# Half of an output projection by seven block products for eight, both token halves together

## The chip, the cores and the metric

The kernel runs on one core of one Trainium2 chip. The metric is the device time of one execution in microseconds (us), as the median of several runs. Profiles show one execution; its engines are named PE (TensorE, matrix products), DVE (VectorE), ACT (ScalarE), POOL (GpSimd) and SP (SyncE, which issues nearly all DMAs here).

## The reference

One decoder layer over 8 sequences of 100 tokens with 1024 features, in float32. Three blocks follow one another, each added to its input and normalised: `x = layernorm(x + block(x))`.

- Retention: 8 heads with 128 features for queries and keys and 256 for values and gates. Its end is what the change touches:

```
o = einsum('bhij,bjhd->bihd', scores, v)
o = o * rsqrt(mean(o*o) + EPS) * g_norm_weight
o = o * (g * sigmoid(g))
return o.reshape(B, T, H * DV) @ Wo          # (800 x 2048) @ (2048 x 1024)
```

- Cross attention with 16 query heads and 4 key/value heads over 722 context tokens and the causal 100 own ones.
- A gated feed-forward block with 4096 hidden features.

## The kernel before

All activations lie with features on the 128 partitions and tokens along the free axis. The 800 tokens are two halves of `N` = 400 (four sequences each), which is the width of nearly every matmul. A float32 operand is split into a high and a low part in the format that TensorE takes (`split2`, L66: a copy on ACT, L67, and a subtraction on DVE, L68); a product of two such operands is three matmuls (`mm3`, L85 to L88: high by high, high by low, low by high).

Weights come through `load_w` (L70): a 512 KB load into one of three `wst` buffers and a split into one of four `w` buffers. The four `big` buffers (L163) hold activations of whichever stage runs.

`seven` (L342) multiplies a 2 x 2 block matrix of weights by a 2 x 2 block matrix of activations with seven block products instead of eight (Winograd's form of Strassen's scheme). The activations' blocks are two feature groups by the two token halves; it needs the operands `b11`, `b21`, `b22` and four mixed ones, `t1` to `t4`, ready and split. The mixtures of the weights are made in the kernel on DVE (L375 to L378). With `into` the results are added on DVE straight into given rows (L360, L369). It is a generator that yields between products, and `in_turn` (L408) interleaves neighbouring units. The retention's projections of heads 1 to 7 and the feed-forward run through it already; one unit is 7 products x 4 x 3 = 84 matmuls.

The retention core of head h (`core`, L475) leaves two tiles `oo[half]`, each with the head's two feature blocks. `gated` (L505) scales them by the root and the gate, splits them and writes high and low parts to the DRAM tensor `o1d` (L516, L517).

The output projection (`out_proj`, L216) runs over the two token halves in turn. `load_o1` (L562) reads the eight heads of one half from `o1d` into four `big` tiles. For each of the 8 row blocks `m` of the result, 16 k tiles accumulate in one PSUM bank: two weight loads (`c` 0: heads 0 to 3, `c` 1: heads 4 to 7) and 48 matmuls. In half 0 the first four row blocks go together, `c` 0 before `c` 1, so that the last heads are needed late. The residual row is added by DVE (L239), the sum for the mean is carried along (L254).

The layer norm of half 0 (`norm_root`, L276, then `scaled`, L269) runs while half 1 is multiplied. For half 1 the mean is taken early, from seven of eight row blocks (`norm_early`, L291, its matmul on L294), while the last row block is multiplied, and corrected by `norm_more` and `norm_late`. The results are the split tiles `z1[half]`, from which the next stage projects queries, keys and values: first four query blocks of half 0, then of half 1. All four `w` buffers are taken by these four blocks. `load_context(0)` (L579) fills the four `big` tiles again in the same stretch, through the `wst` buffers.

The order on each engine is not the program's. A planner runs through the kernel with its own model of times and puts instructions down as they become ready, the earlier ones of the program first; buffers are given out in the same pass. Each engine then works its list off in that order, and SP issues its DMAs in that order too.

Of the kernel before, what the change touches and what calls it, by code (L numbers as in the profile page):

```python
# [8 lines left out]
F32 = mybir.dt.float32  # L9
FR = mybir.dt.float32r  # L10
# [6 lines left out]
P = 128  # L17
# [22 lines left out]
def decoder_layer(ctx, tc, xT, cT, w1, wo1, w2, wo2, wc, w3, wd, gw, qw, kw, trig, dec, mask, out):  # L40
    nc = tc.nc

    def sbuf(name, bufs, side=None):
        return tc.tile_pool(name=name, bufs=bufs, side=side, reuse_waits="tile")
# [21 lines left out]
    def split2(hi, lo, src):  # L66
        nc.scalar.copy(hi, src)  # L67
        nc.vector.tensor_tensor(lo, src, f32(hi), ALU.subtract)  # L68

    def load_w(src, w=None, parts=1):  # L70
        st = wp.tile([P, KT * P], F32, tag="wst", name="wst", bufs=3)
        if w is None:
            w = wp.tile([P, 2, KT * P], FR, tag="w", name="w", bufs=4)
        for i in range(parts):
            c = slice(i * KT * P // parts, (i + 1) * KT * P // parts)
            nc.sync.dma_start(out=st[:, c], in_=src[:, c])
            split(w[:, :, c], st[:, c])
        return w
# [17 lines left out]
    def acc_tag():  # L96
        turn[0] += 1
        return "as"[turn[0] % 2]
# [66 lines left out]
    def big(shape):  # L165
        return bp.tile(shape, FR, tag="big", name="big")
# [49 lines left out]
    def out_proj(half, w, load_o, res, yp, ybufs, p, make_z, dst, after=None):  # L216

        og = load_o(half)
        y = yp.tile([P, KT, N], F32, tag="y", name="y", bufs=ybufs)
        s1 = p.tile([P, N], F32, tag="s1", name="s1", bufs=2)  # L220
        first = 4 if half == 0 else 1
        for ms in [range(first)] + [[m] for m in range(first, KT)]:
            if half == 1 and KT - 1 in ms:
                early = norm_early(y, s1, p)
            accs = [bank(("aaasaaaa", "sssaaass")[half][m])[:, :N] for m in ms]
            for c in range(2):
                for m, acc in zip(ms, accs):
# [24 lines left out]
    def add_up(s1, y, m):  # L252
        if m > 0:
            nc.vector.tensor_tensor(s1, y[:, 0] if m == 1 else s1, y[:, m], ALU.add)  # L254
# [36 lines left out]
    def norm_early(y, s1, p, first=KT - 1):  # L291
        n = y.shape[2]
        mean = bank("s")[:, :n]
        nc.tensor.matmul(mean, onem7, s1, start=True, stop=True)  # L294
# [125 lines left out]


    with sbuf("l1", 2) as p:
# [82 lines left out]
        def gated(h, g):  # L505

            ln_exp()
            rs = [inv_root(p, ss[half], eps_o, pin=True) for half in range(2)]
            for half, r in enumerate(rs):
                t = oo[half]  # L510
                nc.vector.tensor_tensor(t, t, r[:, None, :].to_broadcast([P, 2, N]), ALU.mult)
                for blk in range(2):
                    nc.vector.tensor_tensor(t[:, blk], t[:, blk], g[half, blk], ALU.mult)
                of = p.tile([P, 2, N], FR, tag="of", name="of", bufs=1)
                split2(of, t, t)
                nc.sync.dma_start(out=f32(o1d[h, :, half, :, 0]), in_=f32(of))  # L516
                nc.sync.dma_start(out=f32(o1d[h, :, half, :, 1]), in_=t)  # L517

        def silu(acc, t=None):
            t = temp() if t is None else t  # L520
# [41 lines left out]
    def load_o1(half):  # L562
        t = [big([P, 2, 2, 2, N]) for _ in range(4)]
        for h in range(NH1):
            nc.sync.dma_start(out=f32(t[h // 2][:, h % 2]), in_=f32(o1d[h, :, half]))
        return lambda k: (t[k // 4][:, k // 2 % 2, k % 2, 0], t[k // 4][:, k // 2 % 2, k % 2, 1])
# [363 lines left out]
    class rows:  # L930
# [144 lines left out]
```

## Time and profile before

| | |
|---|---|
| median of 3 runs | 2516.33 us (2516.01 to 2520.12) |
| profiled execution | 2517.7 us, span 2515.9 us |
| mean granted TensorE clock | 0.993 |
| instructions | 37158, of which 14036 matmuls |
| busy: TensorE, VectorE, ScalarE, GpSimd | 2465.4, 1992.2, 1343.5, 481.2 us |
| DMA | 433.96 MB, 172 GB/s over the span |
| first and last matmul of the output projection | 436.9 and 585.5 us |

The profile lists instructions by line and by the program's tile names, without buffer numbers: `a<-big,w` is a matmul into a PSUM bank with the tag `a` that reads a `big` and a `w` tile. Matmuls overlap, so their durations (0.34 us) are longer than the step from one to the next. A name in angle brackets behind an instruction says what ended the engine's idle time before it.

### The profile page before, as it was taken

Reading aid. Unit: us, or ns where it says so; the run is one execution under the profiler, and the core shown is the slowest. Engines: PE = TensorE matmul, PEld = TensorE weight load, DVE = VectorE, ACT = ScalarE, POOL = GpSimd, SP = SyncE. Lnnn points to the kernel's source line nnn. Section 1 sums busy time; section 2 is a strip of 40 time slices with the busy share of each in tenths; the row PEclk is TensorE's granted clock in tenths of the full one; section 3 lists DMA queues with packets and bytes.
Section 4 is the critical chain, followed back from the end, with each engine's and each line's share of the span. In section 5 each row is a group of like instructions: output and inputs, shape, how many; then the busy total and the mean of one; then the engine's idle time right before and its main releaser. Section 6 shows DMA issues by size and latency. Waiting matters only on the chain.

```text
span 2515.9 us, 37158 instructions
## 1 busy us (share of the span) xinstructions
PE 2465.4 (98%) x14036; PEld 2442.0 (97%) x14036; DVE 1992.2 (79%) x3110; ACT 1343.5 (53%) x2264; POOL 481.2 (19%) x234
## 2 busy tenths in 40 slices
PE   8999999999899999999999999999999999999997
PEld 8999999999899999999999999999999999998997
DVE  7678876568989798899999999866987777666656
ACT  6667676335767565556566566533544544432221
POOL 0111111002645334433433433100000000000000
PEclk9999999999999999999999999999999999999999
DMA  7334445774444654554554554574455445388731
GB/s 240 110 110 127 136 144 187 239 266 148 144 152 133 207 175 142 178 166 151 169 176 144 166 192 135 189 273 152 145 181 192 159 160 167 127 302 311 250 102 53
DMA packets 224450, 433.96 MB, mean 172 GB/s; under 512 B 47338, under 2 KB 168042, under 8 KB 211854
## 3 DMA queue, kind: packets, MB, share of 16 engines
q1 hardware_dynamic: 223118, 427.39, 50.7%
q0 software_dynamic: 1152, 4.19, 1.1%
q8 instruction: 110, 1.80, 0.3%
q14 instruction: 70, 0.57, 0.1%
HBM read 322.18 MB, written 109.35 MB: 172 GB/s over the span
## 4 chain that ended last, share of the span: by engine, by line
PE 89%; DVE 6%; ACT 1%; DMA 1%; issue 1%; SPq 0%; DVEq 0%; ACTq 0%
PE a L88 18%; PE a L86 18%; PE a L87 18%; PE s L88 9%; PE s L87 9%; PE s L86 9%; PE v L88 2%; PE v L86 2%; PE v L87 2%; PE s L491 1%; PE s L688 1%; DVE r L120 1%; DVE r L119 1%; PE s L148 1%; DMA tp<-in_xT 1%
## 5 line engine op out<-in xcount | busy, mean ns | idle before, releaser
L86 PE MATMUL a<-big,w 128*128 128x400 f32 (+2 forms) x1808 | 611.4, 339 | 11.7 <-ACT big L67 7.4
L87 PE MATMUL a<-big,w 128*128 128x400 f32 (+2 forms) x1808 | 611.1, 338 | 0.0
L88 PE MATMUL a<-big,w 128*128 128x400 f32 (+2 forms) x1808 | 609.7, 338 | 0.0
L67 ACT CAST w<-wst 128x1024 fp32r<-128x1024 f32 (+1 forms) x231 | 239.2, 1038 | 389.4 <-PE s L88 130.7
L68 DVE TENSOR_TENSOR w<-wst,w 128x1024 fp32r<-128x1024 f32 (+1 forms) x231 | 281.0, 1218 | 117.0 <-ACT w L67 115.1
L86 PEld LDWEIGHTS a<-big,w 128*128 128x128 f32 x1808 | 341.3, 189 | 13.3 <-ACT big L67 7.7
L87 PEld LDWEIGHTS a<-big,w 128*128 128x128 f32 x1808 | 342.0, 189 | 1.3 <-DVE big L68 0.3
L88 PEld LDWEIGHTS a<-big,w 128*128 128x128 f32 x1808 | 342.0, 189 | 0.9 <-DVE w L68 0.2
L86 PE MATMUL s<-big,w 128*128 128x400 f32 x664 | 230.6, 347 | 0.1
L87 PE MATMUL s<-big,w 128*128 128x400 f32 x664 | 229.2, 345 | 0.0
L88 PE MATMUL s<-big,w 128*128 128x400 f32 x664 | 229.1, 346 | 0.0
L125 POOL PARTITION_ALL_REDUCE ss<-sq x56 | 161.1, 2881 | 336.3 <-DMA zd<-y 167.0
L605 POOL PARTITION_ALL_REDUCE kss<-ksq x64 | 173.2, 2706 | 116.4 <-ACT ksq L604 115.7
L86 PE MATMUL a<-z,w 128*128 128x400 f32 x488 | 168.6, 346 | 8.0 <-ACT r L118 4.3
L88 PE MATMUL a<-z,w 128*128 128x400 f32 x488 | 169.4, 348 | 0.7 <-DVE w L68 0.7
L87 PE MATMUL a<-z,w 128*128 128x400 f32 x488 | 169.4, 347 | 0.0
L87 PE MATMUL s<-z,w 128*128 128x400 f32 x400 | 139.1, 348 | 2.4 <-DVE z L68 2.4
L86 PE MATMUL s<-z,w 128*128 128x400 f32 x400 | 139.9, 350 | 0.0
L88 PE MATMUL s<-z,w 128*128 128x400 f32 x400 | 139.4, 348 | 0.0
L722 ACT ACTIVATE s<-s,rk 128x400 f32<-128x400 f32 x160 | 87.7, 591 | 91.9 <-DVE sm L742 65.5
L86 PEld LDWEIGHTS s<-big,w 128*128 128x128 f32 x664 | 124.6, 188 | 1.4 <-ACT w L67 0.4
L87 PEld LDWEIGHTS s<-big,w 128*128 128x128 f32 x664 | 124.6, 188 | 1.1
(330 smaller groups left out, 5650.9 us busy)
## 6 DMA issues: line engine op xcount, KB each, us to landing
wst<-in_w SPq DMA_DIRECT2D x135, 512.0 KB
w<-wcd SPq DMA_DIRECT2D x64, 1024.0 KB
wst<-in_wo SPq DMA_DIRECT2D x64, 512.0 KB
hd<-h SPq DMA_DIRECT2D x12, 1400.0 KB
wst<-in_wd SPq DMA_DIRECT2D x64, 256.0 KB
big<-o1d SPq DMA_DIRECT2D x16, 800.0 KB
qd<-d SPq DMA_DIRECT2D x32, 400.0 KB
q<-qd SPq DMA_DIRECT2D x32, 400.0 KB
```

The costliest lines, as they stand in the source:

```text
L67: nc.scalar.copy(hi, src)
L68: nc.vector.tensor_tensor(lo, src, f32(hi), ALU.subtract)
L86: nc.tensor.matmul(acc, lh, rh, start=start, stop=False, skip_group_check=chain)
L87: nc.tensor.matmul(acc, lh, rl, start=False, stop=False, skip_group_check=chain)
L88: nc.tensor.matmul(acc, ll, rh, start=False, stop=stop, skip_group_check=chain)
L119: nc.vector.scalar_tensor_tensor(q, ss, eps, q, ALU.add, ALU.mult)
L120: nc.vector.scalar_tensor_tensor(q, q, 3.0, r, ALU.subtract, ALU.mult)
L125: nc.gpsimd.partition_all_reduce(y, x, P, op)
L148: nc.tensor.transpose(tr[0:T, b * P:(b + 1) * P], vt[:, b * T:(b + 1) * T], ident)
L491: nc.tensor.matmul(bt(o)[:, b], vv[:, b * P:(b + 1) * P], pf[:, b], start=True, stop=True)
L605: nc.gpsimd.partition_all_reduce(ss[:, at], sq[:, at], P, RED.add)
L722: nc.scalar.activation(sc, sp, AF.Copy, scale=rk[:, c:c + 1])
```

## The change

The k range of the output projection is cut in two.

Heads 0 to 3 keep eight block products: `by_eight` multiplies one token half by their weights, 24 matmuls for each row block, and adds each result to a row that was loaded beforehand with the residual. For half 0 it runs in front, for half 1 at the end. Their weights are loaded once for each half.

Heads 4 to 7 go through `seven`, both token halves together, in four `rows_unit`s of two row blocks each, between the two. The feature blocks of the 2 x 2 scheme are the two 128-feature blocks of a head, and the four heads are the four k tiles of each block product. For these heads `gated` no longer splits. It makes the mixed operands `t1` to `t4` with four subtractions and writes the seven unsplit operands, head by head, to the new DRAM tensor `o1m`. The seven operand tiles are read back during the front half, one after each row block, and split in place. Four of them use the buffers that later hold `z1`, two are `big` tiles, one is a tile of its own.

All rows of the result, of both halves, now lie in four tiles `yt` that are filled with the residual first and added to in three steps. The sums for the mean of half 0 are made after the units. The last row block of half 1, behind which the early mean is taken, has 24 matmuls instead of 48.

```diff
-    o1d = dr.tile([NH1, P, 2, 2, 2, N], FR, name="o1d")
+    o1d = dr.tile([QT, P, 2, 2, 2, N], FR, name="o1d")
+    o1m = dr.tile([7, P, QT, N], F32, name="o1m")
...
                 for blk in range(2):
                     nc.vector.tensor_tensor(t[:, blk], t[:, blk], g[half, blk], ALU.mult)
+                if h >= QT:
+                    continue
                 of = p.tile([P, 2, N], FR, tag="of", name="of", bufs=1)
                 split2(of, t, t)
                 nc.sync.dma_start(out=f32(o1d[h, :, half, :, 0]), in_=f32(of))
                 nc.sync.dma_start(out=f32(o1d[h, :, half, :, 1]), in_=t)
+            if h < QT:
+                return
+
+            b1, b2 = oo[0], oo[1]
+            t1, t2, t4, t3 = g[0, 0], g[1, 1], g[0, 1], b2[:, 0]
+            nc.vector.tensor_tensor(t1, b2[:, 0], b1[:, 0], ALU.subtract)
+            nc.vector.tensor_tensor(t3, b2[:, 1], b2[:, 0], ALU.subtract)
+            nc.vector.tensor_tensor(t2, b2[:, 1], t1, ALU.subtract)
+            nc.vector.tensor_tensor(t4, b1[:, 1], t2, ALU.subtract)
+            to = lambda a, n: o1m[a:a + n, :, h - QT].rearrange("c p n -> p c n")
+            nc.sync.dma_start(out=to(0, 2), in_=b1)
+            nc.sync.dma_start(out=to(2, 2), in_=b2)
+            for i, t in enumerate((t1, t2, t4)):
+                nc.sync.dma_start(out=o1m[4 + i, :, h - QT], in_=t)
...
-        z1 = [out_proj(half, wo1, load_o1, xT, p, 2, p, lambda _: [z1p.tile([P, 2, QT, N], FR, tag="z", name="z")
-                                                                 for _ in range(2)], zd) for half in range(2)]
...
+    def by_eight(y, w, og, half, s1, p, load=None):
+
+        early = None
+        for m in range(KT):
+            if half == 1 and m == KT - 1:
+                early = norm_early(y, s1, p)
+            wt = load_w(w(m))
+            if load is not None:
+                load(m)
+            acc = bank(acc_tag())[:, :N]
+            for k in range(KT):
+                rh, rl = og(k)
+                a = acc if len(rh.shape) == 2 else bt(acc)
+                mmw(a, wt, k, rh, rl, k == 0, k == KT - 1)
+            if early:
+                nc.vector.scalar_tensor_tensor(y[:, m], early[0], -early[2], y[:, m], ALU.mult, ALU.add)
+            nc.vector.tensor_tensor(y[:, m], y[:, m], acc, ALU.add)
+            if half == 1 and not early:
+                add_up(s1, y, m)
+            yield early
...
+        OPS = ("b11", "b21", "t3", "b22", "t1", "t2", "t4")
+        with sbuf("op1", 1) as op:
+            zb = {}
+            tiles = {"b11": lambda: op.tile([P, 2, QT, N], FR, name="ob"), "b22": lambda: big([P, 2, QT, N]),
+                     "t4": lambda: big([P, 2, QT, N])}
+            og = load_o1(0)
+            eight = by_eight(ys[0], lambda m: wo1[m, 0], og, 0, s1[0], p,
+                             lambda m: load_rows(0, m))
+            next(eight)
+            for name in ("b11", "b21", "t2", "t3", "t1", "t4", "b22"):
+                z = zb[name] = tiles.get(name, z1_tile)()
+                nc.sync.dma_start(out=f32(z[:, 1]), in_=o1m[OPS.index(name)])
+                next(eight)
+                split2(z[:, 0], z[:, 1], f32(z[:, 1]))
+            for m in range(KT):
+                load_rows(1, m)
+            og = load_o1(1)
...
+                def then():
+                    for i in (m, m + 1):
+                        add_up(s1[0], ys[0], i)
+                return lambda: seven(op, w(m), w(m + 1), zb, "ass", into=into), then
+
+            in_turn([rows_unit(m) for m in range(0, KT, 2)])
+        z1 = [[z1_tile() for _ in range(2)]]
+        scaled(ys[0], norm_root(ys[0], s1[0], p), lambda m: zd[0, :, m], z1[0])
+        for early in by_eight(ys[1], lambda m: wo1[m, 0], og, 1, s1[1], p):
+            pass
+        z1.append([z1_tile() for _ in range(2)])
+        norm_more(ys[1], early, p, KT - 1)
+        norm_late(ys[1], early, p, lambda m: zd[1, :, m], z1[1])
```

`load_o1` now reads the four heads of one half into two `big` tiles, `load_rows` loads two rows of the residual into `yt`, and `halfrows` lets the norm's functions see one token half of `yt` as before.

More of the change, by code (lines that the diff above doesn't have):

```diff
@@ L560, in decoder_layer, with z1_tile @@
         in_turn([unit(h, i, then) for h in range(1, NH1) for i, then in ((0, after_qk), (2, after_v), (4, after_g))])
[L562 to L566, printed above, removed]
     z1pool = sbuf("z1", 4)
     z1p = z1pool.__enter__()
-    with sbuf("ln1", 1) as p:
-        z1 = [out_proj(half, wo1, load_o1, xT, p, 2, p, lambda _: [z1p.tile([P, 2, QT, N], FR, tag="z", name="z")
-                                                                 for _ in range(2)], zd) for half in range(2)]
+    def z1_tile():
+        return z1p.tile([P, 2, QT, N], FR, tag="z", name="z")
@@ new lines, in decoder_layer, with __init__, __getitem__ @@
+    class halfrows:
+        def __init__(self, tiles, half):
+            self.tiles, self.at, self.shape = tiles, slice(half * N, (half + 1) * N), (P, KT, N)
+        def __getitem__(self, key):
+            return self.tiles[key[1] // 2][:, key[1] % 2, self.at]
+    def by_eight(y, w, og, half, s1, p, load=None):
[17 more added lines that the diff above has]
+            yield early
@@ new lines, in decoder_layer, with load_o1, load_rows, rows_unit @@
+    with sbuf("ln1", 1) as p:
+        yt = [p.tile([P, 2, 2 * N], F32, name=f"y{i}") for i in range(QT)]
+        ys = [halfrows(yt, half) for half in range(2)]
+        s1 = [p.tile([P, N], F32, tag="s1", name="s1", bufs=2) for _ in range(2)]
+        def load_o1(half):
+            t = [big([P, 2, 2, 2, N]) for _ in range(2)]
+            for h in range(QT):
+                nc.sync.dma_start(out=f32(t[h // 2][:, h % 2]), in_=f32(o1d[h, :, half]))
+            return lambda k: (t[k // 4][:, k // 2 % 2, k % 2, 0], t[k // 4][:, k // 2 % 2, k % 2, 1])
+        def load_rows(half, m):
+            if m % 2 == 0:
+                nc.sync.dma_start(out=yt[m // 2][:, :, half * N:(half + 1) * N], in_=xT[half, :, m:m + 2])
+        OPS = ("b11", "b21", "t3", "b22", "t1", "t2", "t4")
[15 more added lines that the diff above has]
+            og = load_o1(1)
+            def rows_unit(m):
+                def w(mm):
+                    v = wo1[mm, 1].rearrange("p (h b c) -> p b h c", b=2, c=P)
+                    return [v[:, i] for i in range(2)]
+                into = {"c%d%d" % (i + 1, j + 1): yt[m // 2][:, i, j * N:(j + 1) * N]
+                        for i in range(2) for j in range(2)}
+                def then():
[10 more added lines that the diff above has]
+        norm_late(ys[1], early, p, lambda m: zd[1, :, m], z1[1])
```

## The prediction

> **What bounds the kernel now.** I read the page first, then the stage table (busy time by windows) from the last retention head to the end of the second stage, then the timelines of TensorE, VectorE and SyncE at the two edges of the output projection, and last the waits.
>
> ```profile
> PE 2465.4 (98%) x14036; PEld 2442.0 (97%) x14036; DVE 1992.2 (79%) x3110; ACT 1343.5 (53%) x2264; POOL 481.2 (19%) x234
> ...
> PE 89%; DVE 6%; ACT 1%; DMA 1%; issue 1%; SPq 0%; DVEq 0%; ACTq 0%
> ```
>
> TensorE sets the span: 98% busy, 89% of the chain that ended last. A matmul taken out of a stretch without gaps is therefore time off the end; one taken out where something else ends the wait is not. The stage table tells the two apart (columns: stretch, PE, PEld, DVE, ACT, POOL busy, granted clock, DMA share, GB/s):
>
> ```profile
> 436.86:475.98 39.12, 39.12 (x217) 39.12 (x217) 19.63 (x26) 17.87 (x24) 2.68 (x2) 1.00 0.78 262
> 475.98:512.00 36.02, 34.95 (x194) 34.62 (x192) 17.95 (x22) 9.44 (x9) 0.00 (x0) 1.00 0.71 231
> ...
> 539.00:576.30 37.30, 36.16 (x200) 35.83 (x199) 21.16 (x29) 9.76 (x10) 0.00 (x0) 1.00 0.61 183
> ...
> 585.50:611.20 25.70, 23.28 (x116) 22.04 (x116) 22.31 (x39) 16.50 (x29) 2.71 (x1) 0.95 0.67 211
> 611.20:718.00 106.80, 94.48 (x493) 92.34 (x492) 104.45 (x146) 75.51 (x146) 59.94 (x20) 0.95 0.40 131
> 718.00:841.00 123.00, 122.11 (x685) 121.34 (x684) 112.17 (x160) 86.70 (x167) 63.95 (x26) 1.00 0.46 155
> ```
>
> The projection (436.9 to 585.5) keeps TensorE full while VectorE is about half busy. Right behind it, from 611 to 718, VectorE is full (104.45 of 106.80) and TensorE loses 12 us. So what the second stage gains depends on when VectorE is done with the projection's layer norm, not on TensorE alone.
>
> One projection matmul, by the timeline of TensorE:
>
> ```profile
> 499.73 0.34 PE L88 MATMUL a<-big,w 128*128 128x400 f32 x1
> ...
> 510.60 0.34 PE L88 MATMUL a<-big,w 128*128 128x400 f32 x1
> 512.30 0.91 PE L279 MATMUL s<-s,onem 128*128 128x400 f32 x2 [1.37 <-DVE s L254]
> ```
>
> 60 steps lie between the first two rows: 10.87 / 60 = 0.1812 us from start to start.
>
> **Taken out: matmuls.** Before: 2 halves x 8 row blocks x 16 k x 3 = 768. After: heads 0 to 3 in `by_eight`, 2 x 8 x 8 x 3 = 384, and four `rows_unit` of 7 products x 4 k x 3 = 336, together 720. 48 x 0.1812 = **8.7 us** of TensorE.
>
> **Added: VectorE work.** The L68 and L369 rows of the feed-forward's down units, which run the same `seven` with `into`, give one unit three splits of 1.22, four mixes of 0.69, a half split of 0.68 and seven adds of 0.57: 11.1 us, against 84 x 0.1812 = 15.2 us of TensorE. Hidden, as there. New besides are the seven operand tiles, split in place at 128x1600:
>
> ```profile
> L68 DVE TENSOR_TENSOR t<-t,h 128x1600 f32<-128x1600 f32 x12 | 21.9, 1824 | 0.9
> L67 ACT CAST h<-t 128x1600 fp32r<-128x1600 f32 x12 | 18.4, 1536 | 11.4 <-DVE t L871 11.3
> ```
>
> That is 7 x 1.82 = 12.8 us of VectorE. It falls between the last gate (about 462) and the second unit's end (about 507): with two units (22.2), half of the eight row adds (8 x 0.57 / 2 = 2.3) and part of the third unit's preparation (up to 7.1) VectorE has 37 to 44 us to do in 45. The old kernel used 4.05 of 14 and 15.71 of 31 us there. It fits, without slack. In stage 1, `gated` of heads 4 to 7 drops two splits (2 x 0.99, and 2 x 0.86 on ACT) and adds four subtractions (4 x 0.57): +0.3 us of VectorE a head, under full TensorE, nothing. Three of the ten `tp` temporaries stay taken until their write has landed, some 9 us longer; the next heads ask for them a unit (15 us) later, so again nothing, and 2 to 3 us a head if that cover were gone.
>
> **DMA.** A head of 4 to 7 writes 1.4 MB for 1.6 MB. The tiles are read as 7 x 0.82 MB where eight half-heads were 6.6 MB. The first loop needs in some 45 us the tiles (5.7 MB), weights (about 4.7), rows of x (3.3), the last head's writes (1.4): 15 MB, 336 GB/s; the old kernel reached 341 in its window 507 to 538. The unit weights come in 512 B rows: in the trace's packet records those take 27 ns (19 B/ns), 4096 B ones 159 ns (25.8 B/ns), so the 4.2 MB of the units cost about 3.6 us more DMA time over 61 us, hidden while the weights are a unit ahead. The Trainium skill ("DMA: Bandwidth & Descriptors", Specifications) has line rate from 512 B on, by which this would be nothing; the records differ, and they decide. On SyncE's queue the tile loads stand among the weight loads, and each must wait for the last head's `o1m` writes; behind a waiting one stand the weights, of which four split tiles (4 x 4.35 us) lie ahead.
>
> **The first edge.** Until the tiles are there TensorE has the front half: 21 projection matmuls before 440.6 as now, all 192 done at 436.9 + (24 + 192) x 0.1812 = 476.0. `b11` needs only half 0 of the gate (done 454.7) and has 10 us of room. `b21` lies where the gate's temporaries lay, so it waits for the writes of `t1`, `t2`, `t4`. Last gate product about 461, four subtractions to 463.4, then a write's landing. The nearest row:
>
> ```profile
> 458.40 0.38 SPq L517 DMA_DIRECT2D o1d<-ot  x1
> 461.15 0.33 SPq L76 DMA_DIRECT2D wst<-in_wo  x1
> 464.77 0.33 SPq L565 DMA_DIRECT2D big<-o1d  x1
> ```
>
> The load of the last head left 6.4 us after the write was issued, and SyncE's waits put 3.2 of them on that write. So 463.4 + 6.4 = 470, the load 4 to 6 us (a 512 KB weight in the chain: 6.27), the two splits 3.4: 477 to 479, needed at 476.0 + 12 x 0.1812 = 478.2. Bounds: 0, and 13 us if the two late tiles queue behind the other five and the weights (8.8 MB at 419 GB/s is 21 us from 470, to 491). I take **+1.0**, near the low end, as the dependent load of the old kernel caused no gap at all.
>
> **The second edge.** `norm_early` of half 1 now starts with 24 matmuls left instead of 48. The old edge:
>
> ```profile
> 576.34 0.83 PE L294 MATMUL s<-s,onem 128*128 128x400 f32 x2
> ...
> 605.20 0.34 PE L86 MATMUL s<-z,w 128*128 128x400 f32 x1
> 607.97 0.45 PE L87 MATMUL s<-z,w 128*128 128x400 f32 x1 [2.42 <-DVE z L68]
> ```
>
> The chain from the mean to the first `z1[1]` tile took 31.6 us, the cover 28.9. With 24 x 0.1812 = 4.35 us less cover and the same chain, 4.35 of the 8.7 are handed back, since VectorE opens the next stage only after that. Against it: eight context splits (3.6 + 3.5 us of VectorE) lie inside this chain, and two of the four `big` tiles they fill come free a whole back half (35 us) earlier now. If half of them move out, 0.8 is handed back. But the norm of half 0, spread over 65 us of matmuls before, now shares 35 us with eight weight splits: about 32 of 35 us of VectorE, so little room to move into. Bounds 0.8 and 4.35; I take **+2.0**.
>
> A gap costs more than itself: behind the 2.77 us one above, matmuls came 0.333 us apart until 611.4 (clock 0.95 in that window), about 1.7 us more. The Trainium skill ("TensorE: Matmul & The Clock Gate", Part 1) wants an idle window of about 3.4 us before the clock halves; the trace shows it after a shorter one. By the rule alone, gaps of 1 to 3 us would cost only themselves.
>
> **Sum.** -8.7 + 1.0 + 2.0 = -5.7 us. The profiled execution took 2517.7 us (span 2515.9, 1.8 around it): 2512.0 on its scale. The median of the runs is 1.4 lower, 2516.33: **2510.6 us**.
>
> **Rivals.** A measurement of this kernel tells about 0.2% (5 us) from no change.
>
> 1. *Handed back.* VectorE, full from 462 to 507 and again in the back half, delays the first units by 3 us and the chain by the whole 4.35: -8.7 + 4.35 + 3 = -1.4, 2515 us. For it: VectorE is already what the next stage waits for, and the change adds 38 us to it (12.8 of tile splits, 16 x 0.69 of mixes, 28 x 0.57 of adds, 2 of weight splits less). Against it: on paper the work fits.
>
> 2. *Late tiles, slower.* One mechanism: write, landing, read and split of the last head's mixed operands in series, with nothing for TensorE between the front half and the first unit, as the back half's operands need `big` tiles that come free only at 476. A gap of 10 us, 2.5 for the halved clock, 2.0 at the second edge: +5.8, 2522 us. It decides from a gap of about 5 us on, where the gain is gone. The down units, with DMA as full, had such a gap once (3.2 us, and the clock at 0.93 in that window):
>
> ```profile
> PE s L86 <- ACT w L67: 3.2, 1, 3.2
> ```
>
> 3. *No saving.* That the products are not fewer is excluded by the count above.
>
> **Chances.** Forecast 0.42 (faster by over 0.2%); handed back 0.28; late tiles 0.30. Best case: nothing handed back and one halved stretch fewer, -10.4, about 2506; the worst that I keep is the 13 us gap, 2525, at the range's end. Range 2505.5 to 2524.5; the forecast's own is 2506 to 2511.
>
> **What will show it.** Right: 720 projection matmuls 0.181 us apart; no TensorE gap above 1.5 us between the last front matmul and the first `b21` product; the mean of half 1 some 4 us earlier than 576.3; z1[1] about 6 us earlier than 608. Wrong: a gap on `ob` or `z` tiles behind a DMA landing near 476 (rival 2), VectorE at 100% over 462 to 507 with TensorE waiting on L68 or L360 (rival 1), or the second stage's window, 611 to 718, losing more than its 12 us. A second stage whose order comes out otherwise could move the time either way by a few us that no step here holds.

## The result, and the profile after

The kernel after took **2534.92 us** as the median of 6 runs (2534.53 to 2535.83); the kernel before, beside it on the same chip, 2519.12. The ratio is 1.0061, 95% interval 1.0046 to 1.0076: **slower by 0.6%**, some 15 us. The prediction was 2510.6 with a range to 2524.5; the kernel became slower instead of faster, and by more than the range allowed.

The first view is the page of the kernel after, busy time by engine and the shares of the chain that ended last:

```profile
PE 2465.0 (97%) x13988; PEld 2438.5 (96%) x13988; DVE 2028.8 (80%) x3169; ACT 1345.0 (53%) x2263; POOL 479.7 (19%) x234
...
PE 84%; DVE 8%; DMA 4%; ACT 2%; issue 1%; SPq 0%; POOL 0%; DVEq 0%; ACTq 0%; POOLq 0%
```

48 matmuls are gone, yet TensorE is as long busy as before (2465.0 against 2465.4): some of the others ran at half the clock (granted 0.989 on the mean, 0.993 before). In the chain TensorE fell from 89% to 84%; VectorE and DMA have gained what it lost. The span of this execution is 2534.1 us (2515.9 before). The stage table shows where (stretch, PE, PEld, DVE, ACT, POOL, clock, DMA share, GB/s):

```profile
436.86:475.98 39.12, 38.86 (x215) 38.56 (x214) 26.33 (x36) 18.96 (x26) 2.74 (x2) 1.00 0.74 240
475.98:512.00 36.02, 27.61 (x135) 25.86 (x134) 28.43 (x33) 13.24 (x11) 0.00 (x0) 0.91 0.86 313
539.00:576.30 37.30, 37.30 (x204) 36.71 (x203) 25.84 (x41) 14.48 (x20) 0.14 (x1) 1.00 0.38 115
585.50:611.20 25.70, 16.52 (x75) 15.21 (x74) 21.58 (x37) 11.32 (x18) 0.00 (x0) 0.80 0.59 174
```

Two stretches lost matmuls: 476 to 512 has 135 where before had 194, and 585 to 611 has 75 where before had 116. The waits of TensorE from 400 to 660 name the two gaps (total us, times, longest):

```profile
PE s L306 <- DVE y L611: 9.2, 1, 9.2
PE s L86 <- ACT w L67: 6.9, 1, 6.9
PE s L86 <- ACT z L67: 3.3, 1, 3.3
PE s L87 <- DVE z L68: 2.5, 1, 2.5
```

**The first gap, 498.59 to 505.83.** The first unit is done, and the second lacks its second weight block. The timeline of SyncE shows why:

```profile
476.56 6.12 SPq L629 DMA_DIRECT2D y<-in_xT  x4
484.35 5.20 SPq L624 DMA_DIRECT2D big<-o1d  x4
490.33 28.13 SPq L332 DMA_DIRECT2D wst<-in_wo  x10
```

Behind the operand tiles SyncE issued the residual rows of half 1 (L629) and the four heads for the back half (L624), and only then, at 490.33, the missing weights (L332). The heads are read only from 550 on. Of the rows the first unit adds to one pair from 492 on; the other three pairs are not needed before the second unit's additions (515). The chain of waits tells the same in order (start, us):

```profile
470.02 8.48 DMA z<-o1m
478.52 12.79 DMA y<-in_xT
491.33 11.74 DMA wst<-in_wo
503.16 0.70 DVE ws L376
```

**The second gap, 594.84 to 604.67.** TensorE's timeline (groups start at the first of their instructions):

```profile
594.48 0.83 PE L295 MATMUL s<-s,onem 128*128 128x400 f32 x2
594.84 0.65 PE L88 MATMUL a<-z,w 128*128 128x400 f32 x1
604.67 1.70 PE L306 MATMUL s<-y,onem 128*128 128x400 f32 x2 [9.18 <-DVE y L611]
605.58 1.14 PE L86 MATMUL s<-z,w 128*128 128x400 f32 x1
```

L295 is the early mean of half 1. It came at 594.48, 18 us later than before, with 47 matmuls of the next stage ahead of it; one matmul later TensorE stands at L306, the correction for the last row block, which needs that mean taken off first. The other 48 matmuls of half 0 wait behind it. VectorE's timeline shows why the mean came late and its subtraction later still:

```profile
590.13 0.56 DVE L255 TENSOR_TENSOR s<-s,y 128x400 f32<-128x400 f32 x1
...
597.26 3.46 DVE L298 SCALAR_TENSOR_TENSOR y<-s,y 128x400 f32<-128x400 f32 x7
```

The last row block that the mean needs was multiplied by 581.6. VectorE, without a pause from 577 to 591, added it at 585.92 and carried the sum along (L255) at 590.13; four splits of context tiles then stand between the sum and the subtraction (L298).

The projection's last matmul started at 585.76, where before had it at 585.52: the first gap has used up the whole saving. The first matmul on z1[1] came at 621.27 (604.84 before). At that point nearly all of the loss is there: 16.4 us, of the 18.2 by which the spans of the two profiled executions differ.

### The profile page after: what moved, and what is told of

Same layout as the page of the kernel before. It is cut to its first block, busy times and chain, and to the rows that moved or that the text cites. A ratio compares the mean times of both kernels' runs of the same rounds, so it can differ in the third digit from the quotient of the medians.

```text
span 2534.1 us, 37102 instructions
## 1 busy us (share of the span) xinstructions
PE 2465.0 (97%) x13988; PEld 2438.5 (96%) x13988; DVE 2028.8 (80%) x3169; ACT 1345.0 (53%) x2263; POOL 479.7 (19%) x234
## 4 chain that ended last, share of the span: by engine, by line
PE 84%; DVE 8%; DMA 4%; ACT 2%; issue 1%; SPq 0%; POOL 0%; DVEq 0%; ACTq 0%; POOLq 0%
PE a L86 16%; PE a L88 16%; PE a L87 16%; PE s L88 9%; PE s L87 9%; PE s L86 9%; PE v L88 2%; PE v L86 2%; PE v L87 2%; DVE r L120 1%; DVE w L68 1%; PE s L785 1%; PE s L492 1%; DVE r L119 1%; DMA wst<-in_wo 1%
## 5 line engine op out<-in xcount | busy, mean ns | idle before, releaser
L86 PE MATMUL a<-big,w 128*128 128x400 f32 (+2 forms) x1728 | 582.6, 338 | 8.7 <-ACT big L67 6.7
L87 PE MATMUL a<-big,w 128*128 128x400 f32 (+2 forms) x1728 | 582.4, 337 | 0.0
L88 PE MATMUL a<-big,w 128*128 128x400 f32 (+2 forms) x1728 | 581.5, 337 | 0.0
L67 ACT CAST w<-wst 128x1024 fp32r<-128x1024 f32 (+1 forms) x223 | 230.7, 1038 | 380.1 <-PE s L88 133.8
L68 DVE TENSOR_TENSOR w<-wst,w 128x1024 fp32r<-128x1024 f32 (+1 forms) x223 | 273.2, 1227 | 102.1 <-ACT w L67 100.6
L86 PEld LDWEIGHTS a<-big,w 128*128 128x128 f32 x1728 | 325.4, 188 | 10.6 <-ACT big L67 6.9
L87 PEld LDWEIGHTS a<-big,w 128*128 128x128 f32 x1728 | 326.0, 189 | 1.3 <-DVE big L68 0.3
L88 PEld LDWEIGHTS a<-big,w 128*128 128x128 f32 x1728 | 326.0, 189 | 1.0 <-DVE w L68 0.2
L86 PE MATMUL s<-big,w 128*128 128x400 f32 x648 | 224.5, 347 | 0.3 <-DMA big<-o2d 0.2
L88 PE MATMUL s<-big,w 128*128 128x400 f32 x648 | 223.8, 346 | 0.0
L87 PE MATMUL s<-big,w 128*128 128x400 f32 x648 | 223.7, 345 | 0.0
L86 PE MATMUL a<-z,w 128*128 128x400 f32 x504 | 174.7, 347 | 7.2 <-ACT d L67 3.6
L88 PE MATMUL a<-z,w 128*128 128x400 f32 x504 | 175.5, 349 | 1.4 <-DVE w L68 1.4
L87 PE MATMUL a<-z,w 128*128 128x400 f32 x504 | 175.3, 348 | 0.0
L86 PE MATMUL s<-z,w 128*128 128x400 f32 x432 | 153.9, 357 | 10.3 <-ACT w L67 6.9
L87 PE MATMUL s<-z,w 128*128 128x400 f32 x432 | 152.2, 352 | 2.5 <-DVE z L68 2.5
L88 PE MATMUL s<-z,w 128*128 128x400 f32 x432 | 151.5, 351 | 0.0
L86 PEld LDWEIGHTS s<-big,w 128*128 128x128 f32 x648 | 121.6, 188 | 1.7 <-DMA big<-o2d 0.5
L87 PEld LDWEIGHTS s<-big,w 128*128 128x128 f32 x648 | 121.6, 188 | 0.8
```

What stands on the lines that cost most here:

```text
L86: nc.tensor.matmul(acc, lh, rh, start=start, stop=False, skip_group_check=chain)
L87: nc.tensor.matmul(acc, lh, rl, start=False, stop=False, skip_group_check=chain)
L88: nc.tensor.matmul(acc, ll, rh, start=False, stop=stop, skip_group_check=chain)
```

## The experiments

Times are medians; ratios are to the kernel before on the same chip, with 95% intervals, and carry the comparisons, since the kernel before took 2515 to 2519 us on the chips that were used. Where an expectation speaks of theories, it says what each of them holds.

### The two gaps, one at a time

**e1: the reads for the back half behind the units.**

```diff
-            og = load_o1(1)
...
             in_turn([rows_unit(m) for m in range(0, KT, 2)])
+            og = load_o1(1)
```

Its four DMAs are kept in the program's order on SyncE's queue.

> The changed kernel with the reads of heads 0 to 3 for half 1 (4 x 0.8 MB) queued behind the last unit's weights instead of in front of the second unit's. Theory A (the 7.1 us gap at 498.6 is the second unit's second weight block, which stands in SyncE's queue and in the DMA engines behind 3.3 MB of reads not needed before the back half): that block is issued some 5 to 6 us earlier, the gap shrinks from 7.1 to under 2 us and the half clock behind it (506 to 513, 3.4 us) goes, so the back half ends 8 to 10 us earlier; the second edge is unchanged: 2525 to 2527 us. Rival B (VectorE's work between 462 and 507 is too much, whatever the DMAs do): gap as before, 2534 us. Rival C (the operand tiles come late): as B, since the tiles are in front of these reads.

Measured: 2526.15 us, 1.0043 (1.0028 to 1.0057). The 7.06 us gap shrank to 2.15, the projection's last matmul came at 580.99, and the second gap stayed (9.09 us, the mean at 589.71). So the position of four reads in one queue moved the projection's end by 4.8 us, not by the 8 to 10 expected. The time lies in the expected range by luck: the kernel before, beside it, was 2.9 us faster than beside the kernel after, and by the ratios the gain is some 5 us.

**e2: the mean of half 1 from six row blocks.** `norm_early` stands before row block 6, `norm_more` follows for 6 and 7.

```diff
-            if half == 1 and m == KT - 1:
-                early = norm_early(y, s1, p)
+            if half == 1 and m == KT - 2:
+                early = norm_early(y, s1, p, m)
...
-            if half == 1 and not early:
+            if early:
+                norm_more(y, early, p, m)
+            elif half == 1:
                 add_up(s1, y, m)
```

> The changed kernel with the early mean of half 1 taken from six row blocks instead of seven, so that 48 matmuls lie behind it as in the kernel before. Theory A (the second edge's 9.7 us gap comes from the mean's place: it stands behind 47 matmuls of the next stage, and TensorE then waits in order for the last row): the mean moves in front of them, the gap of 9.7 and most of the half clock behind it go: -10 to -13 us, 2522 to 2525 us. Rival B (VectorE is full there, and the chain ends when its work is done): the gap moves but z1[1] comes within 3 us of 624.6, 2532 to 2535 us.

Measured: 2525.64 us, 1.0042 (1.0027 to 1.0057). The mean came at 580.82, the gap of 9.65 became one of 2.28, z1[1] came at 613.68, 7.6 us earlier than in the kernel after, and by the ratios some 5 us were gained, less than the 10 to 13 expected. The first gap stayed (7.46). So each gap is real by itself, and neither causes the other.

**e3: the context loads later.** Four context splits stand between the sum for the mean and the subtraction (L298); here `load_context(0)` stands in the queue behind the last store of half 1 (`last`).

```diff
-                    load_context(0)
+                    with tc.issue_after(last[0].ins):
+                        load_context(0)
```

> The changed kernel with the loads of the first context tiles queued behind half 1's stores, so that their eight splits (7.2 us of VectorE, and its 4 us of waits for them) leave the norm's chain. Theory A (place of the mean): only the chain behind the mean gets shorter, z1[1] 6 to 9 us earlier, but the splits come back in the next stage, where VectorE is full: net -2 to -4 us, 2531 to 2533 us. Rival B (VectorE's amount of work): the same work elsewhere on the same full engine, 2534 us or more. If the interposed waits for context data (4 us) are the larger part: -7 us and more.

Measured: 2533.86 us, 1.0073 (1.0057 to 1.009). The gap fell to 5.28 and z1[1] came at 616.92, but TensorE then waited 5.48 us at 639, and from 642 the clock was halved for 10.2 us. By its ratio the run is no faster than the kernel after, as rival B had it. Work pushed out of one full stretch of VectorE fell into the next.

**e4: all three edits.**

> All three edits in the changed kernel: late reads of heads 0 to 3 for half 1, mean from six row blocks, context loads behind half 1's stores. If theory A holds at both edges the gains add up: 2510 to 2514 us, below the kernel before (8.7 us of matmuls come off). If VectorE's amount bounds (rival B): 2530 us or more. If only the first edge can be mended: about 2522 us.

Measured: 2525.3 us, 1.004 (1.0025 to 1.0055), 11 us and more above what was expected. z1[1] came at 604.23, earlier than ever, and a gap of 7.83 us followed at 623.48, where weights wait behind the moved context loads. Edits that each take a gap away do not add up when one of them moves work.

### Both gaps mended

**e12: e1 and e2 together, without e3.**

> The changed kernel with the two edits that each gave 9 us: late reads of heads 0 to 3 for half 1, and the mean of half 1 from six row blocks; the context loads stay where they were. Run with the context loads moved as well, the two gave only 9.6 us together, behind a new gap of 7.8 us for weights at 623.5, which queue behind the moved context loads. If that gap ate the rest (theory A): 2516 to 2518 us, and no gap above 4 us between 595 and 640. If the two edges share one cause, VectorE's amount of work (rival B): 2524 us or more again.

Measured: 2518.55 us, 1.0011 (1.0002 to 1.0021). This is half a us above the expected range, and no gap above 4 us is left between 595 and 640, as expected.

**e12b: besides, the residual rows of half 1 unit by unit.** Rows for the next unit are queued behind the weights of the one before.

```diff
-            for m in range(KT):
-                load_rows(1, m)
+            load_rows(1, 0)
...
+                def make():
+                    if m < KT - 2:
+                        load_rows(1, m + 2)
+                    return seven(op, w(m), w(m + 1), zb, "ass", into=into)
```

> As the kernel with both edits, and each unit's rows of the residual for half 1 (0.4 MB) queued behind the previous unit's weights, so that the second unit's second weight block has 0.4 MB less in front of it. Theory A: the remaining 2.2 us gap at about 500 shrinks by the 1 us that 0.4 MB take, and the half clock behind it (3.4 us, 1.7 lost) may go: 0 to -3 us against the kernel with both edits. Rival B: no difference.

Measured: 2517.7 us, 1.0005 (0.9996 to 1.0015). No gap above 1.1 us is left between the front half and the last unit, and the projection's last matmul comes at 579.30, 6.2 us earlier than before. So queue order and the late mean account for the slowdown within the interval. But the time is that of before: the 6.2 us do not arrive. The rest of the runs look for them.

**f4: does the splitting of the tiles cost anything at the first edge?** e12b without the seven low parts: the copy of each tile on ACT stays, VectorE's subtraction is left out.

> The changed kernel with late reads, late rows and the mean from six row blocks, leaving out the low parts of the seven operand tiles (7 x 1.82 us of VectorE between 475 and 495). It weighs VectorE's load at the first edge: if that costs TensorE time, the gaps of 1.0 and 0.6 us at 477 and 482 and what follows go and the projection ends 1.5 to 4 us earlier than 579.3; if not, within 1 us of it. The time itself: 2516 to 2518 us either way if VectorE bounds the second edge, 2513 to 2515 us if TensorE does.

Measured: 2519.22 us, 1.0015 (1.0006 to 1.0025); the projection ends at 581.41, no earlier. The gaps around the first tiles shrank by 0.8 us together (2.1 to 1.3); then the second unit's weights came later than in e12b and a gap of 2.14 us returned at 500. So of VectorE's 12.8 us there nearly all is hidden, as the prediction had it, and at most about 1 us is not.

**b_early6: the kernel before with the mean from six row blocks.** e2's edit in `out_proj`.

> The kernel before with only the mean of half 1 from six row blocks (96 projection matmuls behind it instead of 48). It tells whether this edit mends the change or would have helped anyway. Theory A (the old cover of 48 missed the chain by 2.6 us): the gaps at 605 to 608 and the half clock behind it go, -3 to -5 us, 2511 to 2513 us. If VectorE's work sets when the next stage starts (rival B): within 2 us of before.

Measured: 2517.1 us, 1.0006 (0.9997 to 1.0015). The mean came 9 us earlier (567.08), but z1[1] was split from 607.87 on (607.35 before), and its first matmul came at 607.01. In the kernel before the mean's time is not what z1[1] waits for.

### Where the saved 6 us go

**e5: the first four context tiles ahead of the back half.** e12b, with `load_context(0, [0])` behind `load_o1(1)`, so that half of the context splits leave the last stretch.

> As the kernel with late rows, and the first four context loads with their splits (3.6 us of VectorE) put before the back half, where two big tiles are free already and VectorE has room (15.3 and 12.4 of 20 us busy at 520 to 560). My own idea was that they leave the norm's chain: z1[1] 3 to 4 us earlier, 2512 to 2515 us. Rival: they take wst buffers from the back half's weights, and TensorE waits there: 2518 us or more.

Measured: 2528.91 us, 1.0055 (1.004 to 1.007). The loads stood in front of the back half's weights on SyncE's queue and in the `wst` buffers: new gaps of 5.98 us at 541 and 2.02 later, and the mean at 586.49. A miss.

**f1: the low parts of the first context on GpSimd.** e12b with:

```diff
-                split(z[k // QT][:, :, k % QT:k % QT + 2, :n], cs)
+                hl = z[k // QT][:, :, k % QT:k % QT + 2, :n]
+                if b > 0:
+                    split(hl, cs)
+                    continue
+                nc.scalar.copy(hl[:, 0], cs)
+                nc.gpsimd.tensor_tensor(hl[:, 1], cs, f32(hl[:, 0]), ALU.subtract)
```

> The changed kernel with late reads, late rows and the mean from six row blocks (2517.7 us, the projection ending 6.2 us earlier than before, but the first result of half 1 at 608.5 as before), and the low parts of the first context tiles (8 splits, 7.2 us of VectorE inside the norm's chain) made on GpSimd, which idles there. If VectorE's amount of work sets when the next stage starts (my theory now): z1[1] 3 to 7 us earlier, 2511 to 2515 us. If the chain's own latency sets it (rival): z1[1] within 1.5 us of 608.5, 2516 to 2519 us.

Measured: 2516.72 us, 1.0005 (0.9995 to 1.0014). The first matmul on z1[1] came 2.1 us earlier than in e12b (603.08 against 605.15), and a later wait for the rotation of the queries grew from 4.02 to 4.85 us: the last matmul in front of the first transposes came at 640.04, against 641.24 in e12b and 641.25 before. So 1.2 us were left there, and none can be told in the time. It is a weak test of the VectorE theory, since some VectorE instructions became slower beside GpSimd (last section).

**f2: the kernel before with the same edit.**

> The kernel before with the same eight low parts on GpSimd, as the control. In it TensorE has no more work that could go earlier than 605, and the old gap there is 2.6 us: by the VectorE theory it gains 2 to 5 us (2511 to 2514 us), mostly in the next stage; by the rival within 2 us of before.

Measured: 2520.1 us, 1.0014 (1.0004 to 1.0023). Slower than before: neither the theory nor the rival has this.

**f3: f1, with the low parts of z1[0] on GpSimd too.**

> As the changed kernel with the context's low parts on GpSimd, and half 0's z1 low parts (8 x 0.49 us of VectorE in the back half) there too. VectorE theory: another 1 to 3 us earlier, 2509 to 2513 us. If GpSimd is slow enough (over 1.5 us for one of 128x400) to delay z1[0], which TensorE needs right behind the projection: a gap there, 2515 us or more.

Measured: 2519.96 us, 1.0017 (1.0008 to 1.0026). GpSimd is too slow for it: the mean of half 1 came at 579.42 behind a gap of 5.61 us.

**g1 and g2: less VectorE in the second stage.** e12b and the kernel before, both with:

```diff
+        if only_cos:
+            nc.vector.tensor_tensor(bt(t1), bt(acc), cosw[:, None, :].to_broadcast([P, NB, T]), ALU.mult)
+            return t1
...
-                        t = rope(p, acc, tb[:, 0], tb[:, 1])
+                        t = rope(p, acc, tb[:, 0], tb[:, 1], only_cos=kv == 0 and i < 4)
```

> The version with all three mends (reads for the back half behind the units, rows of half 1 unit by unit, mean of half 1 from six row blocks), and in the second stage, for the eight query blocks of the first key/value head, the sine half of the rotation left out: the two copies, the multiplication by the sine and the sum, so that these blocks are only multiplied by the cosine. That takes about 8 x (0.94 + 0.91) = 14.8 us of VectorE out of 610 to 700, where it is full. Theory V (what the mended projection gains is handed back because the amount of VectorE's work from 605 to 720 fixes when the second stage's first blocks are done): with that work gone TensorE is the bound there, so the 6.2 us stay: 4 to 7 us faster than the kernel before with the same left out, and 10 to 16 faster than the kernel before itself. Rival O (the pace there is set by something else, the weights' splits, the loads of the context or the planned order): within 2 us of the kernel before with the same left out.

> The kernel before with the same sine half left out for the eight query blocks of the first key/value head: the control of the other run. Theory V: TensorE loses 12 us in its window 611 to 718 and some 2.5 more at half the clock, waiting for VectorE; 5 to 11 us of it go, and the run is 4 to 7 us slower than the mended version with the same left out. Rival O: 0 to 3 us faster than before, if the waits there were not VectorE's, and within 2 us of the mended version.

Measured: 2513.0 us, 0.9986 (0.9978 to 0.9995), for the mended version; 2520.29, 1.0014 (1.0005 to 1.0024), for the control. They parted by 0.28%, 7 us, as theory V said. But the control should have become faster and did not: its waits had only moved (to the transposes at 706 and 772). One half of the expectation right and the other wrong is no proof.

**h1 and h2: four times as much left out.** `only_cos=i < 4`.

> The version with all three mends, with the sine half of the rotation left out for the query blocks of all four key/value heads (32 blocks instead of 8): about 32 x 1.85 = 59 us of VectorE out of 605 to 850, where it has 228 of 245 to do. Theory V (VectorE's amount of work takes the gain back): TensorE is the bound of the whole stage now, and the run is 5 to 8 us faster than the kernel before with the same left out; the first transposed context values come 5 to 7 us earlier than in that run. Rival P (the gain is kept or lost by how the planned order happens to fall, and the 7 us by which the last pair differed were such a fall): the two are within 3 us of each other.

> The kernel before with the sine half left out for the query blocks of all four key/value heads, the control of the other run. Theory V: TensorE's waits for VectorE from 605 to 850, 17 us before, go down to less than 8, so it is 5 to 12 us faster than the kernel before, and 5 to 8 slower than the mended version. Rival P: gaps only change their place, 0 to 5 us faster than before and within 3 us of the mended version.

Measured: 2504.81 us, 0.9955 (0.9941 to 0.9968), mended; 2502.1, 0.9946 (0.9933 to 0.9958), the control. The stage tables of the two, h1 first:

```profile
574.00:610.00 36.00, 29.39 (x136) 26.59 (x137) 32.77 (x57) 18.99 (x33) 0.00 (x0) 0.93 0.57 181
...
660.00:850.00 190.00, 190.00 (x1076) 189.46 (x1075) 146.70 (x212) 107.11 (x210) 95.93 (x40) 1.00 0.51 173
```

```profile
574.00:610.00 36.00, 33.82 (x170) 32.30 (x171) 32.48 (x56) 18.92 (x33) 3.63 (x1) 0.96 0.55 173
...
660.00:850.00 190.00, 189.03 (x1071) 188.34 (x1070) 146.00 (x210) 107.60 (x210) 93.96 (x40) 1.00 0.52 173
```

From 660 on TensorE is full in both, so the sine halves (VectorE's share and their ACT copies) do cost the second stage: the two runs are 11 and 14 us faster than before. But the mended version gained nothing on its control. For the pair that is rival P's outcome, though both runs gained more than it allowed, and theory V fails as the explanation of the 6 us. The 7 us between g1 and g2 would then be the fall of the planned order; no run shows that. The upper rows show where the 6 us are: from 574 to 610, in front of z1[1], TensorE was busy 29.39 us at 0.93 of the clock in the mended version, 33.82 at 0.96 in the control, with 136 matmuls against 170. These 34, at 0.18 us each, are 6.2 us. What the projection had saved was spent there, waiting.

**k1 and k2: h1 and h2 without the low parts of the first context** (a copy of the high part on ACT in their place), to take 7.1 us of VectorE out of the stretch in front of z1[1].

> The mended version with the sine halves left out, and besides the low parts of the eight context tiles of the first sequence left out (a second copy of the high part on ACT stands in for them): 7.1 us less of VectorE between the mean of half 1 and its z1 tiles. Theory S (the gain of the projection is lost at the second edge: the chain on VectorE from the mean of half 1 to z1[1], full with the norm of half 0, weight splits and these context splits, ends at 605 to 609 whatever the projection does, while TensorE has 96 matmuls of half 0 to do): z1[1] starts 4 to 7 us earlier than the 606 to 609 of the run with the sine halves alone, and the time is 3 to 6 us below that run's 2504.8, so level with or up to 3 us below the control. Rival T (z1[1] waits for the deltas and the roots on TensorE and ACT, not for VectorE's amount): z1[1] within 2 us of 606 to 609, and no change of over 2 us.

> The kernel before with the sine halves and the same context low parts left out, the control. Theory S: its z1[1] may be ready earlier too, but TensorE has matmuls of half 0 until 603 there, so only the 2.1 us gap at 604 and the 1.7 us of half clock behind it can go: 0 to 4 us below 2502.1. Rival T: no change of over 2 us.

Measured: 2502.36 us, 0.9948 (0.9933 to 0.9962), and 2498.32, 0.9933 (0.992 to 0.9946). z1[1] was split from 606.63 on (608.59 in h1), and the control's from 603.41 on (605.24 in h2). 2 us instead of the 4 to 7 expected, and in both alike: this is rival T's range for z1[1], while the times fell by 2.5 and 3.8 us, more than it allowed. The copies on ACT had become what VectorE waits for in k1 (its timeline, the idle time in brackets):

```profile
588.95 1.26 DVE L269 TENSOR_TENSOR s<-s,sq 128x400 f32<-128x400 f32 x2 [3.79 <-ACT sq L264]
```

So these two leave open how much the context splits matter. Theory S is neither shown nor excluded in its amount.

## Why the prediction was wrong, step by step

- **Matmuls, -8.7.** Right: 13988 instead of 14036, and 0.18 us apart where the clock was full. The front half ended at 476.60, predicted 476.0. In the projection as a whole the gain went into the first gap.
- **VectorE's added work.** Right in size: the page shows 36.6 us more in all, predicted 38. Between 462 and 507 it was 35.41 of 45, under the 37 to 44 predicted, but the second unit was late and part of its work fell behind 507. f4 shows that the tiles' splits cost at most about 1 us.
- **DMA.** The amount was right: the window from 462 to 507 moved 333 GB/s x 45 = 15.0 MB, as worked out. **The order was the step that failed first.** The text listed what the first loop needs and set it against the rate; it named the tile loads among the weights on SyncE's queue. It did not list what the change puts into that queue ahead of the second unit's weights without needing it yet: three of the four row loads and all four head loads. The channel was 90% busy there (69% in the same window before), and the weights stood last.
- **The first edge, +1.0, bounds 0 to 13.** It was priced at the tiles, and these came nearly in time: the first `b21` product started at 480.74, needed at 478.2, with gaps of 1.20 and 0.61. The unpriced term came one unit later: 7.06 us of waiting for weights, then 4.8 us at 0.333 us a matmul, some 2.2 lost. About 11 us in all, inside the bounds, but mostly from a cause that the text had not named. e1 and e12b show it by taking it away.
- **The second edge, +2.0, bounds 0.8 to 4.35.** The term that was most mis-sized: some 16 us. The bound rested on "the same chain", started by the mean. But the chain starts when VectorE has summed the rows, and VectorE was full with the norm of half 0, which now shares 35 us with the back half. The text had counted "about 32 of 35 us" and concluded only that no context splits could move there, not that the rows would be summed late. The sum (L255) came at 590.13, the mean behind it and behind 47 planned matmuls, and then TensorE's own list held up the 48 matmuls that could have covered the chain. e2 shows the part that the mean's place has: with the mean one row block earlier that gap is 2.28, and z1[1] comes 7.6 us earlier. With both mends (e12b) the first matmul on z1[1] still comes 25.9 us after the projection's last one, where the kernel before has 19.3: the rest of this term is the 6 us that do not arrive.
- **Rival 2, late tiles, 2522.** Its size was near (a gap of 10 and 2.5 for the clock; measured 7.06 and 2.2), its mechanism not: writes and tiles were in time. That it had the kernel slower was right for another reason, so by luck.
- **Rival 1, handed back.** Its result is that of the kernel with both gaps mended, which is level with before. The timeline of VectorE in e12b, whose early mean started at 574.35:

```profile
574.21 1.21 DVE L68 TENSOR_TENSOR w<-wst,w 128x1024 fp32r<-128x1024 f32 x1
575.35 2.99 DVE L68 TENSOR_TENSOR z<-y,z 128x400 fp32r<-128x400 f32 x6
578.26 1.21 DVE L68 TENSOR_TENSOR w<-wst,w 128x1024 fp32r<-128x1024 f32 x1
579.40 1.05 DVE L68 TENSOR_TENSOR z<-y,z 128x400 fp32r<-128x400 f32 x2
580.37 2.97 DVE L298 SCALAR_TENSOR_TENSOR y<-s,y 128x400 f32<-128x400 f32 x6
```

The mean is there, and its subtraction (L298) starts 6.0 us later, behind the splits of half 0's z tiles and of weights. In the kernel before it started 0.9 us after the mean of 576.34:

```profile
577.22 3.46 DVE L297 SCALAR_TENSOR_TENSOR y<-s,y 128x400 f32<-128x400 f32 x7
```

The mean itself is only 2.0 us earlier in e12b, though the projection ends 6.2 earlier, and the subtraction starts 3.2 us later than before. So z1[1] is split from 607.85 on, against 607.35 before: the 6.2 us are gone by then. In h1 and k1 the delay is 6 us again. That VectorE's queue of half 0 is the cause is read from the timeline; no run took it away alone, as f3 made the splits slower instead of moving them. It stays argued, the place is shown.

- **What was to show it.** The 720 matmuls 0.181 us apart: not those behind the first gap. No gap above 1.5 us between the front half and the first `b21` product: held. The mean some 4 us and z1[1] some 6 us earlier: 18 and 16 later. Of the signs of being wrong none came clearly in the place named: TensorE waited no more than 1.2 us at the tiles near 476, and TensorE lost 13.3 us in the window 611 to 718 (106.80 less 93.51), hardly more than the 12 of before. The signs watched the operand tiles and VectorE's total; the loss was in a weight load behind the tiles and in the mean of half 1.
- **The clock.** The trace's price was near: 2.2 us were lost at half the clock behind the first gap and as much behind the second (4.9 us at 0.333 us a matmul). The halved clock lasted 6.8 us with the gap of 7.06, 10.2 with that of 9.65 and 3.4 with the 2.59 in the kernel before; where it lasted longer, it began while TensorE still waited. The Trainium skill ("TensorE: Matmul & The Clock Gate", Part 1) tells of a free-running window of about 3.4 us, and the halved stretches here are its multiples. Its idle bound does not agree with the trace: 2.10 us of idle time in h2 (from 603.58) and 2.28 in h1 (from 584.03) were followed by a halved stretch too, and there the trace decides. A gap of 2.27 us in e12b (from 583.86) left the clock at 1.00, so the length of a gap alone does not tell.

No version that computes everything was faster than the kernel before; e12b and f1 are level with it.

## What to carry to other kernels

When a change adds transfers, list each queue in its new order and ask of every entry when it is needed: the first thing that was late here was a weight load behind loads that nobody needed yet. Work moved into a shorter stretch can delay the start of the next chain even if the engine's total fits; price a chain from the instruction that starts it and what is queued ahead of that on its engine. And before counting a saving in one stage, look at what the next stage waits for: if that is another engine, the saving can end there.

## What the runs showed of the hardware

- Some VectorE instructions slow down beside elementwise work on GpSimd. In f1, from 575 to 605 (groups; mean ns of one), with GpSimd busy on context splits:

```profile
L266 DVE TENSOR_TENSOR s<-s,sq 128x400 f32<-128x400 f32 x4 | 4.9, 1214 | 0.3
L68 DVE TENSOR_TENSOR w<-wst,w 128x1024 fp32r<-128x1024 f32 x2 | 3.2, 1612 | 0.0
```

The same operations took 567 and 1214 ns in e12b, where GpSimd was idle. One by one, the L266 that ran beside a GpSimd split took 1.79 to 2.11 us, those that met none or only 0.4 us of one took 0.57. Other instructions did not slow down: L298 and L317 (563 ns on the mean) took 0.56 us beside GpSimd as well. A split of 0.90 us on VectorE took 1.87 on GpSimd. The four slowed instructions took some 4.9 us more, so moving 7.1 us off VectorE brought z1[1] forward by only 2.1.

- A load's time from issue to landing is not told by how busy the DMA engines are. In the chain above the rows took 12.79 us and the weights 11.74, where a 512 KB weight took 6.27 in the chain of the kernel before (from 158.65); the engines were full in all three (share 1.01 to 1.03). At the rates of these stretches (398, 362 and 297 GB/s) some 5.1, 4.2 and 1.9 MB were moved meanwhile. That the difference is what stood ahead of each load is an estimate from these amounts; e1 agrees with it, where with four reads less in front the weights arrived in time to shorten the gap to 2.15 us.
